# A layer norm's inverse root: a power on GpSimd and two Newton steps in place of a bit guess and three

## The chip, the cores and the metric

The kernel runs on one core of a Trainium2 chip. The metric is the device time of one execution in microseconds (us); of several executions the median is taken. A core has a matrix engine (PE, or TensorE), three engines for elementwise work (DVE or VectorE, ACT or ScalarE, POOL or GpSimd) and a queue engine (SP) that issues DMAs. ACT and POOL can issue DMAs too. Each engine works through its own instruction queue in order; where an instruction needs something that another engine makes, it waits on a semaphore, and everything behind it on its queue waits with it.

## The reference, cut to what matters

Four transformer layers on 32 sequences of 64 tokens of 128 numbers. Each layer has a cross attention (the first: an alignment by dynamic time warping) and a feed-forward part, and each of these eight parts begins with a layer norm of the running sum `x`:

```python
def _layernorm(x, axis=-1, eps=1e-05):
    m = jnp.mean(x, axis=axis, keepdims=True)
    v = jnp.var(x, axis=axis, keepdims=True)
    return (x - m) / jnp.sqrt(v + eps)
...
x = x + _L0_xattn_ref(ctx_1024, _layernorm(x, axis=-1))
x = x + _L0_ffn_ref(_layernorm(x, axis=-1), ...)
x = x + _L1_xattn_ref(ctx_1024, _layernorm(x, axis=-1), ctx_1024, ...)
x = x + _L1_ffn_ref(_layernorm(x, axis=-1), ...)
x = x + _L2_xattn_ref(_layernorm(x, axis=-1), ctx_1024, ctx_1024, mask_Bx1xSxS2_ik0, ...)
x = x + _L2_ffn_ref(_layernorm(x, axis=-1), ...)
x = x + _L3_xattn_ref(_layernorm(x, axis=-1), ctx_1024, ctx_1024, ...)
x = x + _L3_ffn_ref(_layernorm(x, axis=-1), ...)
```

## The kernel before

The 2048 tokens are sixteen tiles of 128 tokens, held for the whole run in four groups `X[0]` to `X[3]` of four tiles each (`TG` = 4). Tokens lie on the 128 partitions, the 128 features along the free axis. A layer norm is done once for each group and each part, so 4 x 8 = 32 times. In the profile its tiles are named after the part: `n` for the parts n0 to n3, n5 and n7, `a2n` and `a3n` for the two attentions of sixteen heads.

One norm (`norm`, line 126) runs on DVE: four `bn_stats` (line 131) and four `bn_aggr` (133) make mean and variance of the four tiles, line 135 adds 1e-5 and leaves `v`, a tile of 128 partitions by 4 columns. `rsqrt` (109) makes `v` to the power -1/2 of it. Four instructions then write the normalised tiles `xl`: on DVE (147), or, after one more small DVE instruction (140), on ACT (142, parts n2 and n3).

`rsqrt` treats the bits of `v` as a whole number, shifts them right by one (112) and subtracts the result from a constant (114), which is a first guess of the root from the exponent. Three Newton steps follow, each of three instructions: `t = y*y` (118), `u = -0.5*t*v` (120), `z = (u + 1.5)*y` (122). All eleven are DVE instructions on 128x4, and each needs the one before it.

What else stands on POOL's queue near a norm is, by line: the squares of the context for the first part (541) and two subtractions for a bias (429); the addition of a bias row to `half1` (941); the loads of the experts' weights (951 and 952), which wait for memory that the part before gives up; the gathers of tokens for the experts (1201) and of the experts' outputs (1220), all indirect DMAs; the addition of a bias row to `X` behind the norms a2n and a3n (776); zeroing of the attention's key buffers (1267, 1397); and products in the last part (1955).

The order on each engine isn't the order of the code alone. The program is scheduled when it is built: of the instructions of one engine that are ready at a modelled time the one that comes first in the code goes next. `in_order` pins an engine to the code's order in some stretches: DVE, ACT, PE, POOL and SP in the first part, PE alone in the others.

Of the kernel before, what the change touches and what calls it, by code (L numbers as in the profile page):

```python
# [15 lines left out]
F32 = mybir.dt.float32  # L16
BF16 = mybir.dt.bfloat16
I32 = mybir.dt.int32
U32 = mybir.dt.uint32
AF = mybir.ActivationFunctionType  # L20
ALU = mybir.AluOpType
AX = mybir.AxisListType

P = 128
# [3 lines left out]
TG = NT // NG  # L28
# [23 lines left out]
def tile_layers(ctx: ExitStack, tc: tile.TileContext, io, out):  # L52
    nc = tc.nc
    keep = ctx.enter_context(tc.tile_pool(name="keep", bufs=1, reuse_waits="tile"))
    small = ctx.enter_context(tc.tile_pool(name="small", bufs=4, reuse_waits="tile"))
# [45 lines left out]
    ident = con[:, C_ID : C_ID + P]  # L101
    ones = keep.tile([P, P], F32, name="ones")
    nc.gpsimd.memset(ones, 1.0)

    table = keep.tile([P, 1], F32, name="table")
    nc.scalar.activation(table, ones[:, :1], AF.Sqrt)
# [1 line left out]

    def rsqrt(v, n, name):

        gi = small.tile([P, n], I32, tag="rs_i", name=f"{name}_i")
        nc.vector.tensor_scalar(gi, v.bitcast(I32), 1, None, ALU.logical_shift_right)
        gj = small.tile([P, n], I32, tag="rs_j", name=f"{name}_j")
        nc.vector.tensor_scalar(gj, gi, -1.0, float(0x5F3759DF), ALU.mult, ALU.add)
        y = gj.bitcast(F32)
        for k in range(3):
            t = small.tile([P, n], F32, tag="rs_t", name=f"{name}_t{k}")
            nc.vector.tensor_tensor(t, y, y, ALU.mult)
            u = small.tile([P, n], F32, tag="rs_u", name=f"{name}_u{k}")
            nc.vector.scalar_tensor_tensor(u, t, -0.5, v, ALU.mult, ALU.mult)  # L120
            z = small.tile([P, n], F32, tag="rs_y", name=f"{name}_y{k}")
            nc.vector.scalar_tensor_tensor(z, u, 1.5, y, ALU.add, ALU.mult)
            y = z
        return y

    def norm(g, name, scalar=False):

        st = small.tile([P, TG, 6], F32, tag="ln_s", name=f"{name}_s{g}")
        mv = small.tile([P, TG, 2], F32, tag="ln_m", name=f"{name}_m{g}")
        for t in range(TG):  # L130
            nc.vector.bn_stats(st[:, t, :], X[g][:, t, :])
        for t in range(TG):
            nc.vector.bn_aggr(mv[:, t, :], st[:, t, :])
        v = small.tile([P, TG], F32, tag="ln_v", name=f"{name}_v{g}")
        nc.vector.tensor_scalar(v, mv[:, :, 1], 1e-5, None, ALU.add)
        r = rsqrt(v, TG, f"{name}_r{g}")
        xl = keep.tile([P, TG, D], F32, tag=f"xl{g}", name=f"{name}_xl{g}")
        if scalar:
            shift = small.tile([P, TG], F32, tag="ln_b", name=f"{name}_b{g}")
            nc.vector.scalar_tensor_tensor(shift, mv[:, :, 0], -1.0, r, ALU.mult, ALU.mult)  # L140
            for t in range(TG):
                nc.scalar.activation(
                    xl[:, t, :], X[g][:, t, :], AF.Identity, bias=shift[:, t : t + 1], scale=r[:, t : t + 1]
                )
            return xl
        for t in range(TG):
            nc.vector.tensor_scalar(  # L147
                xl[:, t, :], X[g][:, t, :], mv[:, t, 0:1], r[:, t : t + 1], ALU.subtract, ALU.mult
            )
        return xl  # L150
# [334 lines left out]
    with tc.tile_pool(name="dtw", bufs=1, reuse_waits="tile") as dp:  # L485
# [28 lines left out]
        for v in (vb1.rearrange("p b a h k -> p (b a h k)"), vb16.rearrange("p b a h k -> p (b a h k)")):  # L514
            n = v.shape[1] // P
# [51 lines left out]
        for h in range(2):  # L567
# [7 lines left out]
            gi = db.tile([P, 512], I32, tag="gi", name=f"gi{h}", bufs=1)  # L575
# [723 lines left out]
    with tc.tile_pool(name="f1w", bufs=2, reuse_waits="tile") as fw, tc.tile_pool(name="f1g", bufs=1, reuse_waits="tile") as fg:  # L1299
# [79 lines left out]
        n = 0  # L1379
# [3 lines left out]
        n = max(n, NS + 5)  # L1383
# [699 lines left out]
```

## Time and profile before

| | |
|---|---|
| median of 6 runs | 1109.01 us (1105.45 to 1117.4) |
| the profiled execution | 1106.55 us, of which its span 1104.8 us |
| DVE busy | 766.7 us, 69% of the span |
| PE busy | 909.8 us, 82% |
| ACT busy | 575.7 us, 52% |
| POOL busy | 153.2 us, 14%, 176 instructions |
| `rsqrt` | 32 calls of 11 DVE instructions on 128x4, medians 0.154 to 0.169 us each |

The page of a profile begins with the busy time of each engine. The chain of waits is followed back from the last instruction: at each step to what released it, or to the instruction before it on its engine, so its pieces add up to the span, and work that isn't on it can grow a little without costing time. The groups list instructions of one line and one shape with their mean duration. The timeline lists instructions in order of time; in square brackets stands how long the engine had been idle, and what ended that. "issue" is time in which the engine waited for nothing that the profile shows.

### The profile page before, as it was taken

To read this page: it belongs to the slowest core of one execution; us is meant where nothing else is said; L and a number is where in the kernel's file an instruction comes from. 1 tells how busy PE (TensorE), PEld (TensorE's weight loads), DVE (VectorE), ACT (ScalarE), POOL (GpSimd) and SP (SyncE) were. 2 spreads that over 40 slices of the span, in tenths; PEclk is the share of its full clock that TensorE was granted. 3 is DMA by queue.
4 is the path that set the end of the run, shared out by engine and by line. 5 is a ranking of instruction groups with operands and counts; after the bars stand their busy time and mean duration, and the time that the engine had idled before them with its cause. 6 is when DMAs were issued, how large, how long until landed. Compare 5 with 4: busy or idle time off the path is not lost.

```text
span 1104.8 us, 26308 instructions
## 1 busy us (share of the span) xinstructions
PE 909.8 (82%) x10816; PEld 678.1 (61%) x10816; DVE 766.7 (69%) x2098; ACT 575.7 (52%) x987; POOL 153.2 (14%) x176
## 2 busy tenths in 40 slices
PE   5668679957578998887747999999999998697987
PEld 3446444445457776444536788888888887354554
DVE  8798887765665437676667777886887757866553
ACT  5545536754243454544446776676776742255542
POOL 3500100020053653500000000000000001200111
PEclk9887979977568999998877999999999999698877
DMA  6733110043221331410000000000000000310000
GB/s 230 180 123 121 69 71 1 20 132 89 75 71 37 62 79 53 115 40 2 1 0 1 2 22 18 6 21 2 22 21 3 3 3 8 93 41 2 10 10 20
DMA packets 63124, 51.89 MB, mean 47 GB/s; under 512 B 32663, under 2 KB 53541, under 8 KB 62878
## 3 DMA queue, kind: packets, MB, share of 16 engines
q1 hardware_dynamic: 46958, 29.86, 9.7%
q0 software_dynamic: 4368, 10.92, 3.8%
q10 hardware_dynamic: 11680, 9.44, 2.6%
q8 instruction: 86, 1.41, 0.5%
q14 instruction: 32, 0.26, 0.1%
HBM read 33.51 MB, written 15.60 MB: 44 GB/s over the span
## 4 chain that ended last, share of the span: by engine, by line
PE 54%; DVE 24%; ACT 9%; DMA 5%; issue 4%; POOL 2%; SPq 1%; ACTq 0%; POOLq 0%; DVEq 0%
PE y L1716 8%; PE po L1735 5%; PE s L1696 4%; PE h L874 4%; PE l L1438 3%; PE h L1327 3%; PE y L1349 3%; DVE lg L1686 2%; PE a_s L1521 2%; PE et L1659 2%; PE a_o L1559 2%; PE a_T L156 2%; PE h1T_T L156 2%; PE w L1951 2%; PE o L1963 1%
## 5 line engine op out<-in xcount | busy, mean ns | idle before, releaser
L1716 PE MATMUL y<-wsm,sl 128*32 128x128 f32 x4096 | 118.4, 273 | 2.5 <-ACT sl L1704 2.5
L1716 PEld LDWEIGHTS y<-wsm,sl 128*32 128x32 f32 x4096 | 109.8, 110 | 10.7 <-issue 6.3
L1704 ACT COPY sl<-s 128x1024 f32<-128x1024 f32 x64 | 62.0, 1022 | 69.5 <-PE s L1696 69.5
L1339 ACT ACTIVATE hT<-h1T_T,b_t 128x128 f32<-128x128 f32 x184 | 52.5, 369 | 62.1 <-PE h1T_T L156 61.1
L776 POOL TENSOR_TENSOR X<-X,rows 128x512 f32<-128x512 f32 x8 | 10.2, 1269 | 483.6 <-DVE a3n_xl L147 435.3
L1735 PE MATMUL po<-ybuf,cT 128*64 128x136 f32 x1024 | 66.4, 282 | 7.5 <-ACT e L1457 7.3
L1530 DVE TENSOR_REDUCE a_x<-a_s 128x16 f32<-128x1024 f32 x32 | 38.9, 1216 | 42.2 <-PE a_s L1521 42.2
L1438 PE MATMUL l<-phi,n_xT 128*128 128x256 f32 x256 | 64.9, 409 | 3.3 <-ACT sl L1704 2.6
L1735 PEld LDWEIGHTS po<-ybuf,cT 128*64 128x64 f32 x1024 | 58.3, 137 | 14.2 <-ACT e L1457 8.6
L1696 PE MATMUL s<-lg,n_xl 64*128 64x256 f32 x512 | 65.1, 389 | 0.5 <-ACT e L1457 0.3
L156 PE MATMUL n_T<-con,n_xl 128*128 128x128 f32 x80 | 22.2, 376 | 48.5 <-DVE n_xl L147 31.6
L1438 PEld LDWEIGHTS l<-phi,n_xT 128*128 128x128 f32 x256 | 51.1, 205 | 15.3 <-issue 4.0
L1749 DVE SCALAR_TENSOR_TENSOR acc<-acc,fac,po 128x128 f32<-128x128 f32 x112 | 31.3, 340 | 41.5 <-PE po L1735 41.5
L1201 POOL DMA_INDIRECT xg<-xn_dram,tok_u x46 | 45.1, 980 | 106.7 <-DVE tok_u L1167 66.1
L1453 ACT COPY lg<-l 128x1024 f32<-128x1024 f32 x32 | 32.6, 1020 | 46.1 <-DVE rm L1450 36.0
L1331 DVE COPY hs<-h 128x512 f32<-128x512 f32 x46 | 31.5, 687 | 36.0 <-PE h L1327 35.6
L1696 PEld LDWEIGHTS s<-lg,n_xl 64*128 64x128 f32 x512 | 47.6, 186 | 12.4 <-issue 5.6
L1533 ACT ACTIVATE a_e<-a_e 128x1024 f32<-128x1024 f32 x32 | 33.8, 1058 | 37.9 <-DVE a_e L1532 37.6
L1544 ACT COPY a_eT<-a_T 128x512 f32<-128x512 f32 x64 | 34.8, 590 | 32.6 <-PE a_T L156 31.8
L1457 ACT ACTIVATE e<-l,nmr 128x256 f32<-128x256 f32 x128 | 50.1, 500 | 0.4 <-DVE nmr L1451 0.4
L1349 PE MATMUL y<-w2e,hT 128*128 x368 | 49.3, 278 | 0.0
L1327 PE MATMUL h<-w1e,xgT 128*128 x92 | 48.6, 616 | 0.8 <-DMA xg<-xn_dram,tok_u 0.7
(406 smaller groups left out, 2144.8 us busy)
## 6 DMA issues: line engine op xcount, KB each, us to landing
vd<-vb ACTq DMA_DIRECT2D x8, 576.0 KB
wsm<-in_W SPq DMA_DIRECT2D x8, 512.0 KB
y_dram<-ys SPq DMA_DIRECT2D x10, 256.0 KB
a2vb<-vd SPq DMA_DIRECT2D x4, 576.0 KB
a3vb<-vd SPq DMA_DIRECT2D x4, 576.0 KB
w1e<-in_W POOLq DMA_DIRECT2D x4, 512.0 KB, 6.8
w2e<-in_W POOLq DMA_DIRECT2D x4, 512.0 KB, 10.1
ctxT<-in_ctxT SPq DMA_DIRECT2D x4, 256.0 KB
```

What stands on the lines that cost most here:

```text
L156: nc.tensor.transpose(ps[:, t * P : (t + 1) * P], a, ident)
L874: nc.tensor.matmul(ps, xp[:, k, 2 * t : 2 * t + 2, :].rearrange("p b s -> p (b s)"), w1k[:, k, :], start=(k == 0), stop=False,)
L1201: nc.gpsimd.indirect_dma_start(gathered[m][:, t, :], None, xn_dram[h][:], bass.IndirectOffsetOnAxis(ap=phase[h]["tok"][:, j : j + 1], axis=0),
L1327: pe_at[0] = nc.tensor.matmul(po, xgT[m][:, t * P : (t + 1) * P], w1f[:, bass.ds(at_e[m][t], 512)], start=True, stop=True)
L1339: nc.scalar.activation(hT[n][:, c, :], ps[:, c * P : (c + 1) * P], AF.Silu, bias=phase[h]["b1"][:, c, j : j + 1])
L1349: nc.tensor.matmul(yo[m][:, t * D : (t + 1) * D], a[:, c, :], w2f[:, bass.ds(at_e[m][t] + c * D, D)], start=(c == 0), stop=(c == 3),)
L1438: nc.tensor.matmul(psv[:, k, :], xT2[g][:, k * P : (k + 1) * P], phi[:, c * CS : (c + 1) * CS], start=True, stop=True,)
L1457: nc.scalar.activation(e[:, k, :], psv[:, k, :], AF.Exp, bias=nmr[:, c, t : t + 1])
L1696: nc.tensor.matmul(ps[r][:, k * CS : (k + 1) * CS], xl2[g][half, k, :], lgs[c, g][half, k, :], start=True, stop=True,)
L1704: nc.scalar.copy(sl[:, r].rearrange("p q s -> p (q s)"), ps[r])
L1716: nc.tensor.matmul(pyv[(n % 4) * 32 : (n % 4) * 32 + 32, b, n // 4, :], sl[:, b % 2, 2 * h + b // 2, n * 32 : n * 32 + 32], wsm[c][:, n, : ...
L1735: nc.tensor.matmul(pov[r * 64 : r * 64 + 64, k // 2, k % 2, :], cT[:, j, at : at + 64], y[:, 2 * k + r, j, :], start=(j == 0), stop=(j == 1),)
```

## The change

A tile of 128x4 with the value -0.5 is set once at the start. `rsqrt` begins with one GpSimd instruction that raises `v` to this power, and takes two Newton steps in place of three. The two DVE instructions of the bit guess are gone.

```diff
     nc.gpsimd.memset(ones, 1.0)
+    minus_half = keep.tile([P, TG], F32, name="minus_half")
+    nc.gpsimd.memset(minus_half, -0.5)
...
-        gi = small.tile([P, n], I32, tag="rs_i", name=f"{name}_i")
-        nc.vector.tensor_scalar(gi, v.bitcast(I32), 1, None, ALU.logical_shift_right)
-        gj = small.tile([P, n], I32, tag="rs_j", name=f"{name}_j")
-        nc.vector.tensor_scalar(gj, gi, -1.0, float(0x5F3759DF), ALU.mult, ALU.add)
-        y = gj.bitcast(F32)
-        for k in range(3):
+        y = small.tile([P, n], F32, tag="rs_i", name=f"{name}_i")
+        nc.gpsimd.tensor_tensor(y, v, minus_half[:, :n], ALU.pow)
+        for k in range(2):
             t = small.tile([P, n], F32, tag="rs_t", name=f"{name}_t{k}")
             nc.vector.tensor_tensor(t, y, y, ALU.mult)
             u = small.tile([P, n], F32, tag="rs_u", name=f"{name}_u{k}")
```

## The prediction

> **What bounds the kernel now.** I read the busy times first, then the chain of waits as a whole, then the chain around each of the 32 norms, then POOL's groups and its timeline.
>
> ```profile
> PE 909.8 (82%) x10816; PEld 678.1 (61%) x10816; DVE 766.7 (69%) x2098; ACT 575.7 (52%) x987; POOL 153.2 (14%) x176
> ...
> PE 54%; DVE 24%; ACT 9%; DMA 5%; issue 4%; POOL 2%; SPq 1%; ACTq 0%; POOLq 0%; DVEq 0%
> ```
>
> PE is on the chain for 54% of the span, DVE for 24%. So what matters is not DVE's busy time but which norms lie on the chain. The pieces of the chain with the lines 112, 114, 118, 120 and 122 add up to 25.6 us. They come in two kinds. Some norms stand alone: each instruction waits for the one before it. This is n5 of the third group:
>
> ```profile
> 546.90 0.18 DVE n_r_j L114
> 547.08 0.02 issue
> 547.11 0.17 DVE n_r_t L118
> 547.28 0.02 issue
> 547.30 0.17 DVE n_r_u L120
> 547.48 0.02 issue
> 547.50 0.17 DVE n_r_y L122
> ```
>
> The columns are start, length, what. A step costs 0.196 us from start to start (547.30 - 547.11 is 0.19; eleven steps take 2.16 us in such norms). Other norms are interleaved with DVE work that has to be done anyway. This is n3 of the first group:
>
> ```profile
> 258.38 0.17 DVE n_r_i L112
> 258.54 1.12 DVE s_x L259
> 259.67 0.07 DVE n_r_j L114
> 259.74 1.18 DVE s L261
> 260.93 0.07 DVE n_r_t L118
> ```
>
> Here a step adds only 0.07 us, and 2.30 us of attention work stand between the first steps.
>
> **What is removed.** Five DVE instructions of 128x4 in each norm (lines 112, 114 and one Newton step): 5 x 0.196 = 0.98 us where the norm stands alone. On the chain, place by place:
> - Alone: n1 first group, a2n second, n5 third and fourth, a3n first. 5 x 0.98 = 4.9 us.
> - Interleaved: n3 first (1.59 us of the chain with its gaps), second (1.62) and third group (0.82), n5 second group (1.54), n5 first with a2n fourth (2.33), n7 first with a3n fourth (2.33). Together 10.2 us, of which 5/11 go: 4.65 us.
> - Partly on it: n0 has 6.14 us of the chain; 2.35 us of that are three steps that were held up (below), and 5/11 of the other 3.8 are 1.7 us. n1 fourth, a2n first and third have 1.1 us together: 0.5 us. Sum 2.2 us.
> - n2, the fourth group of n3, the second and third of a3n, the last three of n7 and the other two of n1 lie beside PE, ACT and DMA work: nothing. What hides them: PE's matmuls of line 874 (156 to 220 us), the 8.42 us landing of `qv` at 241.5, the products of line 1951. Without that cover each would give 0.98 us.
>
> **What is added.** One POOL instruction in each norm, with a wait for DVE before it and a wait of DVE behind it. Line 1955 starts 0.07 us after the ACT copy that it waits for (1078.09 to 1078.16), and a dependent DVE step has a gap of 0.03; so 0.10 us of handing over, plus the power itself. No row shows a power. Its nearest rows:
>
> ```profile
> L776 POOL TENSOR_TENSOR X<-X,rows 128x512 f32<-128x512 f32 x8 | 10.2, 1269 | 483.6 <-DVE a3n_xl L147 435.3 <-DVE a2n_xl L147 43.1 <-DVE a3n_r_t L118 5.1
> ...
> L418 POOL TENSOR_TENSOR w1k<-w1k,w1T_f 128x1536 f32<-128x1536 f32 x1 | 3.4, 3423 | 12.1 <-DVE w1T_f L410 12.1
> ```
>
> From 512 to 1536 columns POOL's two-input instruction grows by 2.15 us: 2.1 ns a column and 0.19 us of its own. Four columns at that rate are 0.20 us: the lower end. A power has to be put together from many steps; if a column of it costs as much as 200 columns of products, four cost 1.7 and the instruction 1.9, say 2.0 us: the upper end, which is my allowance and no row. I take 0.9 us, because a software job of POOL that shows its cost, the issue of an indirect DMA, has rows of 0.94 to 0.98 us (lines 1201 and 1220).
> - Alone: 0.9 + 0.10 = 1.00 us for 0.98 removed, 5 x 0.02 = +0.1 us. At the ends -3.4 and +5.6 us.
> - Interleaved: the DVE work between (1.1 to 1.2 us, lines 259, 261, 1530, 1532) covers the power, so +0. Were there no cover it would be 8 x 1.0 us. At 2.0 us some 0.9 us stick out: +7 us.
> - `minus_half`: a POOL memset of 4 columns (that of 8 columns, line 458, has 0.12 us), before 4.6 us, when DVE still waits for `X[0]`. Nothing.
>
> The trace shows that such company can be dear:
>
> ```profile
> 8.33 1.08 POOL L541 TENSOR_TENSOR csq<-ctxT 128x512 f32<-128x512 f32 x1 [3.36 <-DMA ctxT<-in_ctxT]
> 8.35 0.13 DVE L118 TENSOR_TENSOR n_r_t<-n_r_y 128x4 f32<-128x4 f32 x1
> 8.41 1.01 DVE L118 TENSOR_TENSOR n_r_t<-n_r_j 128x4 f32<-128x4 f32 x1
> ```
>
> The second line 118 instruction takes 1.01 us in place of 0.16, until POOL's ends at 9.41. Lines 120 at 11.21 (1.02 us) and 122 at 12.42 (0.80 us) meet the same. `a_x` (line 1530, 1.22 us) and `a_e`, which read PSUM, aren't stretched beside POOL (1.23 us at 1033.40). So a power can hold up a DVE instruction with two inputs in SBUF for what is left of it, at most 0.9 - 0.16 = 0.74 us. Such instructions are near in n0 (four powers) and beside line 1235 (two): 0 to 4.4 us, I take half, +2.2.
>
> **POOL's queue.** The power stands in line behind what POOL does, and the rest behind it.
>
> ```profile
> 468.90 0.94 POOL L1220 DMA_INDIRECT yg<-y_dram,pu  x1 [0.30 <-issue]
> 470.15 0.95 POOL L1220 DMA_INDIRECT yg<-y_dram,pu  x1 [0.30 <-issue]
> 479.14 1.26 POOL L776 TENSOR_TENSOR X<-X,rows 128x512 f32<-128x512 f32 x1 [8.04 <-DVE a2n_xl L147]
> ```
>
> The gathers run without a pause, 1.25 us apart; `v` of the third a2n is ready at 466.16. If the power goes in between, the gathers behind it, which are on the chain, land 0.9 us later; if behind the last, it starts at 471.1, and DVE, which has attention work for this time, goes on with the norm from 472.0 (it needed until 477.95 before). The same holds for the first a2n (gathers until 434.7). 0 to 2 us for the two, I take 1.0. Elsewhere POOL is idle or off the chain: the second a3n finds it zeroing a buffer until 944.45, but its `v` ends there too (line 135 is held up until 944.47). n2's fourth power can stand behind weight loads issued from 238.9 to 244.6, up to 3.5 us, which the wait for `qv` until 249.9 hides.
>
> **The sum.** +0.1 - 4.65 - 2.2 + 2.2 + 1.0 = -3.55 us. On the profiled execution's 1106.55 us that is 1103.0; the median of the runs is 2.5 us above that execution, so 1109.0 - 3.5 = 1105.5 us.
>
> Two rules of the Trainium skill, each in sentences that nothing above needs. GPSIMD Engine Reference, section 4.1, says that elementwise work of two inputs takes about twice as long on GpSimd as on VectorE; taken at its word a power would be an estimated 2 x 0.161 = 0.32 us and the sum near -8 us, but a power isn't the simple arithmetic it was made for. Section 2.1 says that the first call to a freshly loaded GpSimd routine pays about 6 us for its code; if the power needed that, n0 would lose it and the sum be an estimated +2.5 us. The trace shows no such gap that can be told from a load: POOL's first product (8.33 above) waited for its data.
>
> **The rivals.**
> 1. The power is cheap (0.3 us). For it: POOL's rate of 2.1 ns a column. Against it: nothing here says that a power is one step. Alone 5 x (0.4 - 0.98) = -2.9, interleaved -4.65, partly -2.2, hold-ups 6 x 0.14 / 2 = +0.4, queue +0.4: -9 us, 1100 us.
> 2. The power is dear (2.0 us), on the other side. Place: the wait of line 118 for POOL in every norm, with DVE's queue behind it. Alone +5.6, interleaved -4.65 + 7, partly -2.2, n0's four norms partly uncovered 4 x 0.5 = +2, half of six hold-ups of 1.0 us +2: some +9 us, 1118 us. It decides from about 1.4 us: there alone gives +2.6, interleaved -4.65 + 2.4, partly -2.2, hold-ups and queue +2: about nothing. For it: no bound from above in the trace.
> 3. POOL's queue decides, slower too: powers set behind gathers that wait for PE (line 1220 at 423.8 waited 1.4 us) or for tokens (line 1201, until 310), with DVE shut behind them. Two to four such waits of 2 to 3 us: +8 us, 1117 us. For it: POOL is parked at a weight load for 67 us until 225.0. Against it: line 776 at 441.8 stands ahead of gathers that come earlier in the code, so what is ready goes first.
>
> **How the numbers follow.** Forecast 0.52, rivals 0.20, 0.20 and 0.08. The forecast's own range is 1101 to 1110 (hold-ups 0 to 4.4, queue 0 to 2, power 0.6 to 1.3). A measurement of this kernel can tell some 0.5%, 5.5 us, from no change. Of the forecast's 0.52 I give 0.16 to more than 5.5 us faster, 0.34 to no difference, 0.02 to slower. Faster: 0.16 + 0.20 = 0.36; same 0.34; slower 0.02 + 0.28 = 0.30. The range takes in the rivals, 1096 to 1119 us: beyond it stay a power at its lower end with no hold-up, and several queue waits at once.
>
> **What would show it.** Right: a POOL row of 128x4 near 0.9 us x32; DVE some 30 us less busy; steps alone as long as before from `v` to `xl`, n5's second group shorter by 0.7 us. Wrong: a power of 1.4 us or more; DVE waiting for POOL beyond it (for a gather); a gap before the first power; a chain that changes where there is no norm, which would be the schedule's new order and nothing that I summed.

## The result, and the profile after

The changed kernel takes 1125.81 us (median of 20 runs, 1116.92 to 1135.71), the kernel before 1110.23 (46 runs). The ratio is 1.0128, 95% interval 1.0104 to 1.0152: slower by 14 us (1.28% of 1110; 12 to 17 by the interval), where 3.5 us faster was forecast. The profiled execution took 1122.97 us, its span 1120.8. The busy times of its page, and the shares of its chain of waits:

```profile
PE 923.6 (82%) x10816; PEld 687.2 (61%) x10816; DVE 750.9 (67%) x1938; ACT 578.0 (52%) x989; POOL 186.6 (17%) x209
...
PE 53%; DVE 22%; ACT 11%; issue 4%; DMA 4%; POOL 3%; SPq 1%; ACTq 0%; POOLq 0%; DVEq 0%
```

DVE has 160 instructions fewer and leaves part of the chain (24% before), POOL comes in (2% before). Nothing here says where the kernel lost 14 us. The groups of the power, with count, busy time, and mean ns of one:

```profile
L114 POOL TENSOR_TENSOR n_r_i<-n_v,minus_half 128x4 f32<-128x4 f32 x24 | 24.3, 1016 | 271.9 <-DVE n_v L134 271.9
...
L114 POOL TENSOR_TENSOR a3n_r_i<-a3n_v,minus_half 128x4 f32<-128x4 f32 x4 | 4.0, 1009 | 379.8 <-DVE a3n_v L134 378.6
```

A power takes 1.01 us, near the 0.9 us that was forecast. So its length isn't where the prediction broke. (Lines of the changed kernel are one lower than before where they lie behind the change: `v` is line 134, the first Newton step's `t` 117. The experiments have lines of their own; the text names what they are.) A norm that stands alone, n5 of the third group, in the timeline (start, length, engine, line; in brackets idle time and its releaser):

```profile
555.52 1.01 POOL L114 TENSOR_TENSOR n_r_i<-n_v,minus_half 128x4 f32<-128x4 f32 x1 [16.31 <-DVE n_v L134]
556.56 0.22 DVE L117 TENSOR_TENSOR n_r_t<-n_r_i 128x4 f32<-128x4 f32 x1 [0.75 <-POOL n_r_i L114]
```

`v` ended at 555.37: 0.15 us to POOL, 1.01 on it, 0.03 back. From the start of `v` to that of `xl` a norm with nothing in between takes 2.51 to 2.56 us, against 2.38 to 2.39 before. (This one takes 2.53 against 2.63: in both traces a DVE instruction of 0.42 us for `a2o` lies inside, and now it runs while POOL has the power.)

To find where the time went I matched the instructions of PE, ACT and DVE with their like in the trace of before and took the median delay in each stretch of the run (the ledger, from here on). The delay grows at five places: +2.1 us by 20 us (n0), +3.9 from 110 to 140 us (no norm there), +2.6 at 150 to 180 (n1), +5.1 at 310 to 320 (n3), +8 at 940 to 960 (a3n). It shrinks by 3.6 at 500 to 550 (n5). At n2 it grows by 3 and shrinks again by 2.8 where the stage waits for a load; at the third a2n it grows and is gone 20 us later.

The largest step shows most. The part a3n begins with two zeroings of `a3kb`, 3.5 us each, on POOL; 16 loads into it follow on SP, and the scores `a_s` wait for those. POOL's timeline, before:

```profile
937.48 6.96 POOL L1267 MEMSET a3kb<- 128x4096 f32 x2
```

and after:

```profile
937.38 1.01 POOL L114 TENSOR_TENSOR a3n_r_i<-a3n_v,minus_half 128x4 f32<-128x4 f32 x1 [367.31 <-DVE a3n_v L134]
...
951.78 1.02 POOL L114 TENSOR_TENSOR a3n_r_i<-a3n_v,minus_half 128x4 f32<-128x4 f32 x1 [7.46 <-DVE a3n_v L134]
953.97 1.01 POOL L114 TENSOR_TENSOR a3n_r_i<-a3n_v,minus_half 128x4 f32<-128x4 f32 x1 [1.17 <-DVE a3n_r_u L119]
954.93 6.96 POOL L1266 MEMSET a3kb<- 128x4096 f32 x2
```

The first a3n's `v` begins at 927.78 before and at 937.07 after. The zeroings begin 9.7 us behind it before, 17.9 us after. Before, they start as the bias row ahead of them on POOL's queue ends (line 776, from 936.28 for 1.27 us). After, the same row is done at 944.32 (942.94 and 1.38 us). But the powers of the second and third norm stand between it and the zeroings, and their `v` comes only at 951 and 953. No power waits here for longer than the 0.15 us of handing over. What waits is the work behind them, and it is on the chain of waits. Before (start, length, what):

```profile
937.48 3.52 POOL a3kb L1267
...
951.47 2.17 DMA a3kb<-kd
953.69 2.00 PE a_s L1521 x6
```

and after:

```profile
954.93 3.52 POOL a3kb L1266
...
968.91 2.15 DMA a3kb<-kd
971.11 1.99 PE a_s L1520 x6
```

My theory from this (the queue theory): the loss is made by the order on POOL's queue, by powers that stand behind slow work and by work that stands behind powers whose `v` comes late. Two rivals: the price (a power with its handing over costs more on the path than the five instructions it replaces), and the clock (the granted clock of PE from 112 to 140 us is 0.89 in the one trace and 0.70 in the other; perhaps any new timing upsets it).

### The profile page after: what moved, and what is told of

The parts are those of the page before. It is cut to its first block, busy times and chain, and to the rows that moved or that the text cites. A ratio compares the mean times of both kernels' runs of the same rounds, so it can differ in the third digit from the quotient of the medians.

```text
span 1120.8 us, 26193 instructions
## 1 busy us (share of the span) xinstructions
PE 923.6 (82%) x10816; PEld 687.2 (61%) x10816; DVE 750.9 (67%) x1938; ACT 578.0 (52%) x989; POOL 186.6 (17%) x209
## 4 chain that ended last, share of the span: by engine, by line
PE 53%; DVE 22%; ACT 11%; issue 4%; DMA 4%; POOL 3%; SPq 1%; ACTq 0%; POOLq 0%; DVEq 0%
PE y L1715 7%; PE po L1734 5%; PE s L1695 4%; PE l L1437 3%; PE h L1326 3%; PE y L1348 3%; PE a_s L1520 3%; DVE lg L1685 2%; PE a_o L1558 2%; PE a_T L155 2%; PE h L873 2%; PE et L1658 2%; PE h1T_T L155 2%; PE o L1962 1%; DVE rm L1449 1%
## 5 line engine op out<-in xcount | busy, mean ns | idle before, releaser
L114 POOL TENSOR_TENSOR n_r_i<-n_v,minus_half 128x4 f32<-128x4 f32 x24 | 24.3, 1016 | 271.9 <-DVE n_v L134 271.9
L114 POOL TENSOR_TENSOR a3n_r_i<-a3n_v,minus_half 128x4 f32<-128x4 f32 x4 | 4.0, 1009 | 379.8 <-DVE a3n_v L134 378.6
```

## The experiments

In each run the kernel before ran on the same chip, and ratios are to that. Four of the runs (22 powers; n0, n1, and n2 with a2n undone) fell on a chip where the kernel before took 1123 us. All four of their traces lose some 11 us between 456 and 480 us, where PE stands still again and again, and no trace from another chip does. There too only ratios are compared, but what these runs say of that stretch is weaker.

**Two Newton steps, no power.** In the kernel before:

```diff
-        for k in range(3):
+        for k in range(2):
```

> The kernel before, with its third Newton step left out (so the root is coarser); no power, and nothing new on GpSimd, whose order of work is that of before. Queue theory (the loss of the changed kernel is made by where the powers stand in GpSimd's queue): 96 small VectorE instructions fewer and nothing added, so 2 to 6 us below before, about 1104 to 1108. Price theory (a power with its handing over costs more on the path than the instructions it replaces): also below before, 1104 to 1108. Reorder and clock theory (any change of the instructions' timing upsets the granted clock, as between 112 and 140 us, where it was 0.89 before and 0.69 after): the clock there may fall here too, and the time be 1110 to 1118.

1105.26 us, ratio 0.9948 (0.9926 to 0.9969). Taking DVE instructions away is worth 5.8 us where nothing is put on POOL (at the price of a coarser root).

**A short instruction in the power's place.**

```diff
-        y = gj.bitcast(F32)
-        for k in range(3):
+        y = small.tile([P, n], F32, tag="rs_p", name=f"{name}_p")
+        nc.gpsimd.tensor_tensor(y, gj.bitcast(F32), ones[:, :n], ALU.mult)
+        for k in range(2):
```

> The guess from the exponent stays on VectorE, then GpSimd multiplies it by one (128x4, in place of the power and at its place in the queue), then two Newton steps (the third is left out). Queue theory: what stands ahead of it on GpSimd is as in the changed kernel, so the waits at n0, n1, n3, a2n and the late zeroings stay, less where the two VectorE instructions shift the order: 1118 to 1126, near the changed kernel, although the instruction itself takes perhaps a third of the power's 1.0 us. Price theory: a short instruction makes the loss go away, 1106 to 1112.

1124.84 us, ratio 1.0118 (1.0089 to 1.0147): all but the whole loss, although the instruction takes 0.20 us in place of 1.01. This is the run that tells price from queue. n0 shows how that can be; POOL's timeline in the changed kernel:

```profile
6.08 1.02 POOL L114 TENSOR_TENSOR n_r_i<-n_v,minus_half 128x4 f32<-128x4 f32 x1 [1.07 <-DVE n_v L134]
10.76 1.21 POOL L428 TENSOR_TENSOR cb<-cb,cb 1x512 f32<-1x512 f32 x1 [3.66 <-ACT cb L425]
11.93 2.03 POOL L540 TENSOR_TENSOR csq<-ctxT 128x512 f32<-128x512 f32 x2
13.92 1.14 POOL L428 TENSOR_TENSOR cb<-cb,cb 1x512 f32<-1x512 f32 x1
15.03 2.96 POOL L114 TENSOR_TENSOR n_r_i<-n_v,minus_half 128x4 f32<-128x4 f32 x3
```

and with the multiplication:

```profile
14.18 1.15 POOL L430 TENSOR_TENSOR cb<-cb,cb 1x512 f32<-1x512 f32 x1
15.29 0.50 POOL L116 TENSOR_TENSOR n_r_p<-n_r_j,ones 128x4 f32<-128x4 f32 x3
```

Three of n0's norms have their `v` between 7.1 and 9.3 us. Their power starts at 15.03 because a `cb` that waits for ACT, two `csq` and another `cb` are ahead, and the multiplication starts at 15.29 for the same reason. The first `csq`, at 8.33 before, is now behind a `cb` and starts at 11.93. By its ledger the run with the multiplication loses 3.2 us at n0, 4.1 at n3 and 6.6 at a3n, with 0.20 us in place of 1.01. Not every place is the same: at n1 it loses nothing, and it has 3.7 us at 1010 us that belong to the clock (below). So the total is as large, but not made of the same pieces throughout.

**The a3n part undone, and its order alone.** The first keeps the guess and three steps in the four a3n norms, by a choice in `rsqrt` that the later runs use with other names:

```diff
-        y = small.tile([P, n], F32, tag="rs_i", name=f"{name}_i")
-        nc.gpsimd.tensor_tensor(y, v, minus_half[:, :n], ALU.pow)
-        for k in range(2):
+        if name.split("_")[0] in ('n0', 'n1', 'n2', 'n3', 'a2n', 'n5', 'n7'):
+            y = small.tile([P, n], F32, tag="rs_i", name=f"{name}_i")
+            nc.gpsimd.tensor_tensor(y, v, minus_half[:, :n], ALU.pow)
+            steps = 2
+        else:
...
+            y = gj.bitcast(F32)
+            steps = 3
+        for k in range(steps):
```

The second keeps every power and ties three of them behind the zeroings by an edge that only the build's scheduler sees:

```diff
-        nc.gpsimd.tensor_tensor(y, v, minus_half[:, :n], ALU.pow)
+        power = nc.gpsimd.tensor_tensor(y, v, minus_half[:, :n], ALU.pow)
+        if zeroed and name.startswith("a3n"):
+            tc.add_manual_dep(power.ins, zeroed[-1].ins.name, ...)
...
-            nc.gpsimd.memset(kb, 0.0)
+            zeroed.append(nc.gpsimd.memset(kb, 0.0))
```

> The changed kernel, with the guess and three steps kept in the four a3n norms alone. Queue theory: the two 3.5 us zeroings of a3kb no longer stand behind the powers of the second and third a3n, so they begin about 10 us after the first a3n's v as before (18 us in the changed kernel), and the 8 us lost at 940 to 950 us come back: about 1117, 8 below the changed kernel. Price theory: four powers fewer are worth 4 times 0.2 us, about 1125. Clock theory: no difference, 1120 to 1130.

> The changed kernel, with every power kept; only the order on GpSimd is changed at one place: the powers of the second to fourth a3n stand behind the two zeroings of a3kb and not ahead of them. Queue theory: the zeroings begin some 10 us after the first a3n's v and the 8 us lost at 940 to 950 us come back, less what the second a3n's power waits for the zeroings' end (0 to 2 us): 1117 to 1120. Price theory: the same powers are on the same path, 1125 and no change. Clock theory: no change, 1120 to 1130.

1117.41 us, ratio 1.0053 (1.0026 to 1.0081), and 1116.35 us, ratio 1.0028 (0.9991 to 1.0065). POOL's timeline of the second:

```profile
934.73 1.01 POOL L116 TENSOR_TENSOR a3n_r_i<-a3n_v,minus_half 128x4 f32<-128x4 f32 x1 [367.38 <-DVE a3n_v L143]
...
941.62 6.96 POOL L1275 MEMSET a3kb<- 128x4096 f32 x2
949.13 2.07 POOL L116 TENSOR_TENSOR a3n_r_i<-a3n_v,minus_half 128x4 f32<-128x4 f32 x2 [0.55 <-DVE a3n_v L143]
```

The zeroings start 7.2 us after the first `v` (934.42), and neither later power waits for them. The same 32 powers in another order are some 11 us cheaper (1.0128 - 1.0028 = 0.0100). In its ledger the step at 940 to 960 us is gone (6.6 before it, 6.3 behind it). The price theory allowed nothing here.

**24 powers.** The edge of the run before, and the guess with three steps back in the eight norms whose power had waited 2.5 to 7.9 us:

```diff
+        if name in ('n0_r1', 'n0_r2', 'n0_r3', 'n1_r1', 'n1_r2', 'n1_r3', 'n3_r3', 'a2n_r2'):
...
+            return newton(gj.bitcast(F32), v, n, name, 3)
```

> The changed kernel with the power kept in 24 of the 32 norms, those whose power found GpSimd free (waits of 0.08 to 0.16 us after v); the guess and three steps are back in the eight that it made wait 2.5 to 7.9 us (n0 and n1 second to fourth, n3 fourth, a2n third), and the zeroings of a3kb stand ahead of the a3n powers. Queue theory: nothing is left of the loss, and what the prediction summed for the rest shows, 2 to 5 us below before: 1105 to 1109, ratio 0.995 to 0.998. Price theory: 24 powers at 0.2 us over what they replace, 1111 to 1116, ratio 1.000 to 1.005. Clock theory (time comes from a granted clock that any new timing upsets): 1115 to 1125.

1107.30 us, ratio 0.9971 (0.9934 to 1.0008), where the queue theory put it: 17 us under the changed kernel, not told from the kernel before, and below what the price theory allowed for but for the interval's end.

**n0 with n1, and n3, undone.** The list of names in `rsqrt`, first without n0 and n1, then without n3.

> The changed kernel with the guess and three steps back in the eight norms of n0 and n1; all else as in the changed kernel. Queue theory: the powers behind csq and cb at 14 to 17 us and behind phi, bsm and xpad at 165 us cost 2.1 and 2.7 us by the two traces, so 1119 to 1123, some 4 to 5 below the changed kernel. Price theory: 8 powers of 32, 1 us at most, 1124 to 1126.

> The changed kernel with the guess and three steps back in the four norms of n3. Queue theory: the fourth norm's power stood behind nine gathers of xg for 5.8 us, and its removal gives back 5.1 us at 310 to 320 us, less 0.8 us that the first three gain by the power: 1120 to 1123, 3 to 5 below the changed kernel. Price theory: 0.5 us at most, 1125.

1.0035 (1.0004 to 1.0066) and 1.0070 (1.0039 to 1.0101): 10 and 6 us back, where 4 to 5 and 3 to 5 were expected. With the a3n part's 8 to 11 these are 25 to 28 us and more than the loss.

**The power in n5 and n7 alone.** The list of names is `('n5', 'n7')`.

> The kernel before, with the power and two steps in the eight norms of n5 and n7 alone, where GpSimd has nothing else. Queue theory and the prediction's own sum: n5 gains 3.6 us by the two traces, n7 up to 1: 3 to 4 us below before, 1107 to 1108, ratio 0.996 to 0.998. Price theory: 8 powers at 0.2 us over what they replace, less the interleaved ones, 1110 to 1113.

1109.12 us (median of eleven runs; a twelfth took 2896.73 and is left out), ratio 0.9992 (0.9962 to 1.0021): not told from no change, so the 3 to 4 us weren't shown. Its trace has a gain at n5 (the delay falls by 4.2 us from 520 to 550), but the trace of a kernel with the old norms there (the power in n1 alone, below) gets 3.0 us later from 500 to 550, so a single trace can't show it.

**Which of the pieces overlap.** n0, n1, and n2 with a2n taken out of the list of names; and the run with 24 powers, with `n0_r0` and `n1_r0` added to its list.

> The changed kernel with the guess and three steps back in n0 alone. Undoing n0 and n1 together gave back some 10 us, where the traces showed 4.7 us of waiting; this and the next run ask from which of the two the rest comes. Queue theory: 2.1 us back, and more if the late start of n0 is what leaves the granted clock low up to 150 us (0.880 over the whole run, 0.886 with n0 and n1 undone): ratio 1.011 by the wait alone, 1.006 if the clock goes with it. Price theory: 1.012.

> The changed kernel with the guess and three steps back in n1 alone. Queue theory: the 2.7 us at 165 us come back, ratio 1.010, and no more unless the granted clock follows n1. Price theory: 1.012.

> The changed kernel with the guess and three steps back in n2 and a2n: the places where the ledger of the two traces shows a delay that is given back soon after (n2: 3 us lost at 195 to 235 and 2.8 won back at 240 to 250 where the stage waits for a load; a2n third: its power waits 5.0 us behind gathers, of which 0.5 is left 20 us later). Queue theory: these waits are covered, so nothing changes, ratio 1.011 to 1.014. A theory by which every wait of a power counts in full: 3 plus 5 us back, ratio 1.005 to 1.007. Price theory: 8 powers, 1.010 to 1.012.

> As the run with 24 powers, but the guess and three steps are back in the first norm of n0 and of n1 too: 22 powers, and GpSimd's order up to n2 is that of before. In the run with 24 powers the first csq stood behind the first power and a cb and began at 12.05 us (8.33 before), and the stage from 20 to 90 us was 2 to 3.6 us late although no power waited there. Queue theory: that comes back, 2 to 3 us under the run with 24 powers, ratio 0.993 to 0.996. Price theory: two powers fewer, 0.4 us, ratio 0.997. Clock theory: no direction, 0.995 to 1.005.

1.0064 (1.0031 to 1.0097), 1.0048 (1.0015 to 1.0081), 1.0128 (1.0070 to 1.0187), 1.0022 (0.9986 to 1.0059). Undoing n2 and a2n gives nothing back, as expected for places that are covered, and the first ledger says the same (a power of a2n that waits 5.0 us leaves 0.5 us). The run alone would not settle it: its interval ends at 1.0070, where a full count of these waits was put, and a2n lies in the stretch that is slow on this chip. But n0 alone and n1 alone give back 7 and 9 us, where both gave 10. And 22 powers weren't better than 24. The trace of 22 is 0.9 us ahead of that of 24 in the stage from 20 to 100 us, not 2 to 3: n0's first power costs little, and I had read a difference between two executions as one between two kernels. The run of 22 also loses 7.5 us from 310 to 345 us, in stops of ACT where no power stands (the run of 24: 1.6), so which of the two is better stays open.

**One place at a time.** The kernel before, with the power and two steps in the named norms alone.

> The kernel before with the power and two steps in the four norms of n0 alone. Queue theory: three powers wait some 7.5 us behind cb and csq and the first csq is late by 3.6 us, but most of it is covered by the load of w1T; the stage from 20 to 90 us is 0.5 to 2 us late: ratio 1.0005 to 1.002, and 1.004 to 1.006 if the granted clock up to 150 us goes with it. Price theory: 4 powers at 0.2 us, 1.0007.

> The kernel before with the power and two steps in the four norms of n1 alone. Queue theory: the powers of the second to fourth wait 2.5 to 2.8 us behind phi, bsm and xpad and the chain waits with them: 2.7 us, ratio 1.0025. Price theory: 1.0007.

> The kernel before with the power and two steps in the four norms of n3 alone. Queue theory: the first three gain 0.8 us, the fourth loses 5.1 behind the gathers of xg: 4.3 us, ratio 1.004. Price theory: faster by 0.8 us but for 0.2 each, 0.999 to 1.0005.

> The kernel before with the power and two steps in the four norms of a3n alone. Queue theory: the powers of the second and third stand ahead of the zeroings of a3kb, which begin some 18 us after the first a3n's v in place of 10: 7 to 8 us, ratio 1.006 to 1.007. Price theory: 1.0007.

| power in | us | ratio (interval) | us by the ratio |
|---|---|---|---|
| n0 | 1114.84 | 1.0033 (1.0006 to 1.0060) | +3.7 |
| n1 | 1113.08 | 1.0004 (0.9981 to 1.0028) | +0.4 |
| n3 | 1118.30 | 1.0050 (1.0020 to 1.0079) | +5.6 |
| a3n | 1121.07 | 1.0086 (1.0057 to 1.0115) | +9.6 |

The a3n trace is the cleanest: it is within 0.4 us of that of before from 120 to 930 us, then late by 7.1 at 960 to 980 and by 9.9 at the end. The last step, 3.6 us at 1006 to 1014, isn't the queue's: the traces with the power in n0 alone and in n3 alone have it too (7.2 to 10.8, 8.1 to 11.7), without a power there. In all three the granted clock is 0.54 to 0.55 over these 20 us, and 0.76 over the same work in the trace of before (16 us). So of the 9.6 us some 7 are shown to be the zeroings. n3 shows the other way in which the queue costs. POOL issues nine gathers ahead of the fourth norm's power. The chain of waits (start, length, what) with the power in n3 alone:

```profile
325.45 1.06 POOL n_r_i L115
...
326.53 0.18 DVE n_r_t L126
...
327.79 0.70 DVE hs L1339
...
328.54 0.66 PE h1T_T L164 x4
```

and before:

```profile
318.23 3.62 PE h L1327 x4
321.85 0.44 PE h1T_T L156 x4
```

What is late isn't the norm. DVE stands at the norm's `t` until the power is done, and behind it stands `hs`, which the experts' transposes on PE need: 328.54 in place of 321.85. The delay grows from 3.6 to 8.3 us here and stays so up to 1000 us.

n1 explains part of the overlap. With the power in both n0 and n1, and in n1 alone:

```profile
164.26 0.62 POOL L749 DMA_DIRECT2D phi<-in_phi  x1 [15.37 <-DVE n_s L130]
...
165.52 3.00 POOL L114 TENSOR_TENSOR n_r_i<-n_v,minus_half 128x4 f32<-128x4 f32 x3
```

```profile
156.62 0.62 POOL L758 DMA_DIRECT2D phi<-in_phi  x1 [13.18 <-PE al L729]
...
157.87 3.01 POOL L115 TENSOR_TENSOR n_r_i<-n_v,minus_half 128x4 f32<-128x4 f32 x3
```

The three powers stand behind the load of `phi` in both. By the releasers in the brackets `phi` goes in the second when PE is done with `al`, and in the first only when DVE has done statistics of n1 itself. The schedule is another one as soon as n0 has powers too. So n1's 2.6 us are lost only with both changed. In the traces with n0 alone or n1 alone undone the delay doesn't grow there (4.1 to 3.9 us and 2.2 to 2.1 from 150 to 180), so undoing either brings them back. That is 2.6 of the 6 us by which 7 and 9 exceed 10; the rest is not explained, and each of the two runs is known to 3.7 us only.

The clock theory's own place, 110 to 140 us, is answered by two traces of this set whose kernels are that of before up to 250 us, but for the one memset of `minus_half`. The windows of the run (us, then busy times and counts of PE, PE loads, DVE, ACT, POOL, granted clock, DMA share, GB/s), with the power in a3n alone:

```profile
110.00:150.00 40.00, 26.21 (x246) 19.34 (x243) 32.82 (x166) 18.66 (x35) 4.10 (x3) 0.87 0.18 70
```

and in n3 alone:

```profile
110.00:150.00 40.00, 29.35 (x264) 23.49 (x260) 29.65 (x157) 17.41 (x31) 4.11 (x3) 0.74 0.15 55
```

The one is 0.1 us late at 150 us, the other 4.8, and no power has run in either. Of the eighteen traces fifteen have 0.74 to 0.76 in this window; before has 0.88, a3n alone 0.87, n5 with n7 0.84. So it is the trace of before that is the rare one here. The 3.9 us that the first ledger showed there may be one execution's clock, and can't be put down to the powers.

## Why the prediction was wrong, by its own steps

**The step that failed** is POOL's queue, in the sentence "Elsewhere POOL is idle or off the chain". It priced the queue at +1.0 us, at the a2n gathers alone, of which no cost shows (undoing n2 and a2n left the ratio at 1.0128). The prediction had written that "the rest" stands behind the power, and it looked at the second a3n and the zeroings. It took for granted that the power comes behind them, as the zeroing runs until 944.45. In fact the scheduler set two powers ahead of the zeroings, and these with their 16 loads came 8 us late. With the power in a3n alone 9.6 us were lost (6.3 to 12.8), 7.1 of them at this place.

**The fourth n3 at nothing.** It was named among the norms beside other work, but none of the three covers that the prediction then lists lies at 310 to 330 us. Measured: 5.6 us for n3 (2.2 to 8.8), 4.7 of them at this place by the ledger. The norm itself had time, but what is queued behind its first Newton step on DVE had not: DVE waits 6.71 us for POOL there, and the sum had nothing for `hs`. A wait of DVE for POOL beyond the power was among the prediction's own signs of being wrong. The rival with POOL's queue (0.08, 1117 us) had this mechanism, even the gathers of line 1201, but not the zeroings.

**n0 at 1.7 us gained, half of the hold-ups lost.** Measured: 3.7 us lost (0.7 to 6.7). Three powers behind `cb` and `csq`, and the first `csq` 3.6 us late, were not in it. For n1 the sum had small gains at the first and fourth norm and nothing at the other two; with n0 changed as well the last three cost 2.6 us by the trace.

**The power, 0.9 + 0.10 us**: 1.01 and 0.18. The five norms alone take 0.13, 0.18, 0.17 and 0.15 us more and 0.10 less from `v` to `xl`, together +0.5 us where +0.1 stood. Right in kind, and small. It also settles the two rivals about a cheap and a dear power. The Trainium skill's page GPSIMD Engine Reference, section 4.1, would have had an estimated 0.32 us by its factor of two on VectorE; the measured 1.01 us is six times the 0.16 us of a DVE instruction here. Its section 2.1, about 6 us for a freshly loaded routine, shows nothing in n0: the first power starts 0.08 us after its `v` and takes 1.02 us.

**The interleaved norms, -4.65 us**: n5 gave 3.6 us by the ledger of the two traces and 4.2 in the run with n5 and n7 alone, more than the 1.8 us which the sum had for n5, but the times of that run don't tell it from nothing. (n5's second group is shorter by 2.41 us from `v` to `xl`, 3.62 for 6.03, not by 0.7: two other DVE instructions now stand inside it in place of five.) Two Newton steps alone gave 5.8 us, so the saving on DVE is real. The powers' places cost more than it brings.

**The hold-ups, +2.2 us**, weren't there. The timeline of the changed kernel's DVE in n0, while POOL runs three powers from 15.03 to 17.99:

```profile
16.07 0.16 DVE L117 TENSOR_TENSOR n_r_t<-n_r_i 128x4 f32<-128x4 f32 x1 [2.03 <-POOL n_r_i L114]
16.27 0.16 DVE L119 SCALAR_TENSOR_TENSOR n_r_u<-n_r_t,n_v 128x4 f32<-128x4 f32 x1
16.46 0.16 DVE L121 SCALAR_TENSOR_TENSOR n_r_y<-n_r_u,n_r_i 128x4 f32<-128x4 f32 x1
```

Steps with two inputs in SBUF keep their 0.16 us beside a power; 18 instructions of the steps lie wholly beside one in this trace, and all take 0.15 to 0.16. Beside a `csq` or a `cb` they took 0.80 to 1.02 in the trace of before, and in the changed kernel they run when the `csq` are done. One alone is stretched, 1.25 us at 962.65, beside a bias row of 128x512. (The prediction's row for instructions that read PSUM, `a_x` at 1033.40, shows little: the product on POOL ends at 1033.43.)

**DVE 30 us less busy**: 15.8. Part of the difference is overlap: two Newton steps alone, 96 instructions fewer, made DVE 13.1 us less busy (753.6), 0.14 each, so 160 would make 22. Another part is the zeroings again; with them ahead of the powers DVE is busy for 747.5 us, 3.4 less. Late as they are in the changed kernel, they meet DVE's own work; its timeline:

```profile
955.69 6.28 DVE L146 TENSOR_SCALAR a3n_xl<-X,a3n_m,a3n_r_y 128x128 f32<-128x128 f32 x1
955.95 6.03 DVE L1805 SCALAR_TENSOR_TENSOR X<-acc,f2z,X 128x128 f32<-128x128 f32 x4
```

Before, instructions of these two lines take 0.34 us each. Here `xl` ends only as the second zeroing does (961.89), and the `X` behind it in DVE's queue with it. In the trace of before other instructions ran beside the zeroings (937.48 to 944.44):

```profile
939.47 1.13 DVE L1806 SCALAR_TENSOR_TENSOR X<-acc,f2z,X 128x128 f32<-128x128 f32 x4
...
942.02 2.45 DVE L135 TENSOR_SCALAR a3n_v<-a3n_m 128x4 f32<-128x4 f32 x1
```

The same `X` goes through unhindered, and a `v` is held until 944.47. So it is the TENSOR_SCALAR of `xl` that a zeroing shuts out. (One of 128x1 passes, in 0.14 us, in the run with the zeroings first.)

**What stays open.** The four places by themselves sum to 19 us, with n1's 2.6 on top and n5's gain against them, more than the 14 us (12 to 17) of the whole; each is known to some 3 us only, so the split is less sure than the sum. And not all of the loss is waiting. Between runs of one kernel 0.01 of the mean granted clock goes with 8.2 us (a line through the runs of the first eight experiments, of before and of after, each kernel with its own level). The changed kernel's runs have 0.880 on average, those of before 0.887, which is 5.6 us by that line, and 24 powers in their places 0.888. The runs with the power in a3n alone have 0.882, some 4 us by the line, about what the step at 1010 us took in the one trace of theirs. So the lower clock seems to come with the late stages, but no run here shows by what.

## What to carry to other kernels

An instruction moved to an idle engine is priced at the two ends of that engine's queue: what can stand ahead of it, and what will stand behind it if its input is late. Both are decided by the scheduler and not by the share of busy time, so read the built order at every place where it lands before reading durations. If a short instruction in the same place costs as much as a long one, it is the place that has to change: one edge of order gave back some 11 of 14 us, and taking the work away without moving it (two Newton steps, 0.9948, with a coarser root) beat both kernels.

## What the runs showed of the hardware

- POOL's power of 128x4 takes 1.01 us, its product of the same shape 0.20 us (four columns in both).
- DVE to POOL takes 0.08 to 0.16 us from the end of `v` to the start of the power where POOL is free, POOL to DVE 0.03 us.
- A power of 128x4 on POOL holds up no DVE step with two inputs in SBUF (0.16 us each beside it); a `csq` of 128x512 held them up to its end in the trace of before (1.01 us in place of 0.16).
- A zeroing on POOL (two of 128x4096, 3.5 us each) holds a DVE TENSOR_SCALAR of 128x128 or 128x4 for all that is left of it (6.28 us of `xl`, 2.45 of `v`; one of 128x1 took 0.14 us beside it), while a SCALAR_TENSOR_TENSOR with two inputs in SBUF passes (four in 1.13 us). The prediction had hold-ups for two-input instructions alone. The Trainium skill's page SBUF — State Buffer, section Who interferes with whom, says both: two SBUF inputs contend only with a POOL instruction that reads SBUF, and TENSOR_SCALAR can take a two-port mode that contends with any. Both fit the zeroings and the `csq`. By the first a power, which reads two tiles in SBUF, should have held the steps too; the 18 beside one kept 0.15 to 0.16 us, so here the measurement differs from the page.
- Kernels with the same program up to 250 us were 0.1 and 4.8 us late at 150 us, at granted clocks of 0.87 and 0.74 from 110 to 150. A ledger of two single traces can't place anything smaller.
